# Sorting layer 2 of one entry and layer 3 of another in the same VectorE instructions

## The chip, the cores and the metric

The kernel runs on one core of a Trainium2 chip. The metric is the device time of one execution in microseconds. A core has five engines that work from queues of their own: TensorE (PE in the profile; its weight loads are listed apart as PEld), VectorE (DVE), ScalarE (ACT), GpSimd (POOL) and SyncE (SP), which here only issues DMAs. Each engine takes its instructions in order, and they wait for each other through semaphores.

## What is computed

Sixteen independent entries, each a graph with N = 1024 nodes, C = 64 features a node, and a weighted adjacency matrix of 1024 x 1024. Four layers run one after another, each followed by a residual and a layer norm:

```python
x = layernorm(x + L0(x, adj))                 # adj @ x, two small dense layers, tanh
x = layernorm(x + (adj / clip(adj.sum(2), 1)) @ x)
x = layernorm(x + L2(x, adj, mask))
x = layernorm(x + L3(x, adj, mask))           # as L2, with other weights
```

L2 and L3 aggregate sorted neighbour values:

```python
adj_ = where(eye, 1.0, adj);  nb = (adj_ > 0) & ~eye;  m = nb.sum(-1)
skip = where(m > 10, (m + 1) // 2, 1)
removed = nb & (skip > 1) & (rank % skip == skip - 1)      # rank: place in the row's list of neighbours
valid = where(removed | removed.T, 0, adj_) > 0
s = sort(where(valid[..., None], x[:, None], big), axis=2) # each channel of each node by itself
agg = sum(w * quantile(s, tau) for tau, w in ((.25,.25), (.5,.5), (.75,.25)))
out = relu((x + agg) @ W1 + b1) @ W2 + b2                  # 64 -> 128 -> 64
return out * mask
```

The lists of neighbours depend on the adjacency alone. So layers 2 and 3 of an entry use the same lists, but layer 3 sorts the values that layer 2 has produced.

## The kernel before, in words

**Tiles.** The 1024 nodes of an entry are sorted by their number of neighbours and cut into 8 tiles of 128 nodes (one node a partition). Tile t has room for SIZES[t] values a node: 10, 11, 13, 14, 15, 17, 19, and 33 for tile 7, the *tail*. A tile of values is `got`, 128 x SIZES[t] x 64 in fp32; slot 0 is the node itself, the other slots are its neighbours.

**How a tile is filled.** Tiles 6 to 0 are filled by GpSimd: `fetch` copies slot 0 (L831) and issues one indirect DMA a slot (`gather`, L333), each of which brings 128 rows of 64 values from a table in DRAM (`table[0]` holds x after layer 1, `table[1]` x after layer 2). The tail is filled by `fill`: for each of its 32 slots VectorE makes a one-hot matrix `hot` out of `place` (is_equal), and TensorE multiplies it with the three bf16 parts of x (24 matmuls a slot, `pick`, L329, into `pgk`); ScalarE copies eight slots at a time to `got` (L690).

**How a tile is sorted.** A network of exchanges, laid down ahead by `exchange_plan`. Each step is one VectorE instruction, min or max of two views of `got` and its partner `other`. All VectorE instructions go through a helper, so that they all have line L197 in the profile. Their free size is (slots in the view) x 64: 64 to 1024 elements.

**What follows.** `weigh`: ScalarE multiplies the wanted slots with the weights of the node (L702, `prods`), and VectorE adds them up to `agg`. When a sort's eight tiles are summed, `finish` runs the MLP (`pt`, `ph`, `pd` on TensorE), the residual and the layer norm (`settle`). In layer 2 the result x3s is scattered to `table[1]` by GpSimd (8 indirect DMAs, L747), read back in the nodes' own order by a DMA of SP (L755), and split into three bf16 parts `x3p` (`split`: casts on ScalarE, L361, L365 and L369, with two VectorE subtractions between them). In layer 3 the result x4s is scattered to the output (8 indirect DMAs, L747).

**What is prepared.** `features` computes layers 0 and 1 of an entry: it reads the adjacency twice, a 128-row strip at a time (issued by SP; L403 `px` and L432 `pa` are its matmuls), and makes `near`, the 0/1 matrix of neighbours, on VectorE beside the first reading. `lists` finds the neighbours to be dropped (L484 `pr`), and `left`, the remaining ones with their number; sorts the nodes; and turns the matrix into lists of indices `idx` (L567 `pk`, and maxima of eight on VectorE). `ordered` moves x, place and the weights into the sorted order.

**What sets the order.** The loops are Python generators. The order of the instructions on VectorE, ScalarE and TensorE is written out as they are called (`manual_schedule`); GpSimd and SP get theirs from the framework's scheduler. `Weave` interleaves the generators: each `yield` names a delay, counted in estimated VectorE time, before the generator may go on. The sort itself is the main line; after each of its instructions `catch_up` lets those generators step that are due. `weave.finish(gen)` runs a generator to its end on the spot.

**The main line before.** For each k, `phase(k, 0)` sorts layer 2 of entry k, and `phase(k-1, 1)` sorts layer 3 of entry k-1. At its start a phase completes the filling of its own tail, completes what the filling of the next phase's tail needs, and starts that one. Tiles 6 to 0 are fetched three tiles ahead, into four buffers (`got_s`); there are two tail buffers (`got_l`), five `hot` and three `prods`.

Of the kernel before, what the change touches and what calls it, by code (L numbers as in the profile page):

```python
# [21 lines left out]
P = 128  # L22
# [7 lines left out]
HOTS = 5  # L30
# [59 lines left out]
def cut(t, view, shift=0):  # L90
    s, m, stride, o, length = view
    s += shift
    if m == 1:
        return t[:, s + o : s + o + length, :]
    return t[:, s : s + m * stride, :].rearrange("p (m s) w -> p m s w", m=m)[:, :, o : o + length, :]

# [106 lines left out]
def adj_resnorm_kernel(ctx: ExitStack, tc: tile.TileContext, x, adj_t, nodemask, w01, b01, w02, b02,  # L203
# [20 lines left out]
    off_diag = const.tile([P, P], BF, name="off_diag")  # L224
# [71 lines left out]
    wants = [wanted(low, k) for low, k in zip(LEAST, SIZES)]  # L296
    usual = [exchange_plan(k, want) for k, want in zip(SIZES, wants)]
# [75 lines left out]
    def features(b, e):  # L373
# [3 lines left out]
        near = s.sets.tile([P, NT, N], BF, name="near")  # L377
# [15 lines left out]
        for h in range(NH):  # L393
# [5 lines left out]
            for q in range(G):  # L399
                t = h * G + q  # L400
                rows = slice(t * P, (t + 1) * P)
                for jt in range(NT):
                    nc.tensor.matmul(px[C:, q * P : (q + 1) * P], x_s[:, jt, :], adj[t][:, jt, :], start=jt == 0,  # L403
                                     stop=jt == NT - 1)
                if q == 1:
                    nc.scalar.copy(node_in[:C], px[:C])  # L406
                yield 5
                dve.tensor_scalar(near[:, :, rows], adj[t], 0.0, None, op0=ALU.is_gt)
                dve.tensor_mul(near[:, t, rows], near[:, t, rows], off_diag)
                load(t + 2)  # L410
# [5 lines left out]
            hid_t = s.work.tile([C, HALF], F32, name="hid_t", bufs=1)  # L416
# [7 lines left out]
        e.near = near  # L424
        dve.tensor_add(y, y, b02r[:, None, :].to_broadcast([P, NT, C]))
        yield from settle(x1[:, :, :C], y, "x")
        for h in range(NH):
            pa = s.psum.tile([P, G, C + 1], F32, name="pa", tag="x", bufs=1)
            for q in range(G):
                i = NT + h * G + q  # L430
                for jt in range(NT):
                    nc.tensor.matmul(pa[:, q, :], adj[i][:, jt, :], x1[:, jt, :], start=jt == 0, stop=jt == NT - 1)  # L432
                yield 5
                load(i + 2)
# [4 lines left out]
            dve.tensor_mul(y[:, h * G : (h + 1) * G], pa[:, :, :C], deg[:, 1, :, None].to_broadcast([P, G, C]))  # L439
        x2 = s.feat.tile([P, NT, C], F32, name="x2", tag="x_s", bufs=1)  # L440
# [3 lines left out]
        while b >= 2 and entries[b - 2].tail[0] is None:  # L444
            yield 2
# [4 lines left out]
    def lists(b, e):  # L450
# [26 lines left out]
        for t in range(NT + 1):  # L477
# [8 lines left out]
            yield 4  # L486
            if t:
                for i in range(2):
                    junk = s.work.tile([P, N], BF, name="junk", bufs=1)
                    nc.scalar.activation(junk, prs[t - 1], AF.Sign, bias=lim[:, i, t - 1 : t], scale=-1.0,  # L490
                                         accum_out=cut_at[:, i, t - 1 : t])
            yield 2.5
# [16 lines left out]


        left = s.sets.tile([P, NT, N], F16, name="left")
# [3 lines left out]
        for t in range(NT + 1):  # L515
            if t < NT:
                rows = slice(t * P, (t + 1) * P)
                pv = s.psum.tile([P, N], F32, name="pv", tag="big", bufs=2)
                pvs.append(pv)
# [5 lines left out]
            yield 4  # L525
            if t:
                nc.scalar.activation(left[:, t - 1, :], pvs[t - 1], AF.Relu)  # L527
                junk = s.work.tile([P, N], BF, name="junk", bufs=1)
                nc.scalar.activation(junk, left[:, t - 1, :], AF.Sign, accum_out=key[:, 4, t - 1 : t])
            yield 2  # L530
        e.left = left
# [11 lines left out]
        for t in range(NT):  # L543
            junk = s.work.tile([P, N], BF, name="junk", bufs=1)
# [14 lines left out]
        e.idx = s.feat.tile([P, NT, KS], I32, name="idx", bufs=4)  # L559
        pks, codes, found = {}, {}, []  # L560
        for t in (*reversed(range(NT)), -1, -2, -3):
            if t >= 0:
                pk = pks[t] = s.psum.tile([P, N], F32, name="pk", tag="big", bufs=2)
                for h in range(NH):
                    cols = slice(h * HALF, (h + 1) * HALF)
                    for c in range(NT):
                        nc.tensor.matmul(pk[:, cols], order[:, c, t * P : (t + 1) * P], left[:, c, cols],  # L567
                                         start=c == 0, stop=c == NT - 1)
            yield 4
# [8 lines left out]
            yield 3  # L578
# [13 lines left out]
    def ordered(b, e, order, own):  # L592
# [17 lines left out]
        e.rows = s.feat.tile([P, NT], I32, name="rows", bufs=5)  # L610
        dve.tensor_copy(e.rows, sorted_own[:, :, 1])
        e.out_rows = s.feat.tile([P, NT], I32, name="out_rows", bufs=5)
        dve.tensor_scalar(e.out_rows, sorted_own[:, :, 1], float(b * N), None, op0=ALU.add)
        e.mask = s.feat.tile([P, NT], F32, name="mask_s", bufs=5)
# [3 lines left out]
        yield 7  # L618
        e.xs[0] = s.feat.tile([P, NT, C], F32, name="x2s", bufs=3)
# [9 lines left out]
        while b >= 3 and entries[b - 3].tail[1] is None:  # L629
            yield 2  # L630
        place = s.feat.tile([P, NT, P], F16, name="place", bufs=3)
# [17 lines left out]
        e.none = s.feat.tile([KW - 1, P], BF, name="none", bufs=4)  # L649
        dve.tensor_scalar(e.none, tail_count, nth[: KW - 1], BIG, op0=ALU.is_le, op1=ALU.mult)  # L650
        e.wts = s.feat.tile([P, NT, KW], F32, name="wts", bufs=4)
        hats(e.wts, [P, NT, KW], n1, slot[:, None, :KW].to_broadcast([P, NT, KW]))
# [19 lines left out]
    def fill(e, layer):  # L672

        t = NT - 1
        size = SIZES[t]
        got = s.lists.tile([P, size, C], F32, name="got", tag="got_l", bufs=2)
        nc.gpsimd.tensor_copy(got[:, 0, :], e.xs[layer][:, t, :])
        for g in range(1, size, 8):
            pg = s.psum.tile([P, 8, C], F32, name="pgk", tag="f", bufs=1)
            for k in range(g, g + 8):  # L680
                hot = s.lists.tile([P, NT, P], BF, name="hot", bufs=HOTS)
                dve.tensor_scalar(hot, e.place, float(k), None, op0=ALU.is_equal)
                whole = k < LEAST[t]
                if not whole:
                    nc.tensor.matmul(pg[:, k - g, :], e.none, ident_b[: KW - 1, k - 1 : k].to_broadcast([KW - 1, C]),  # L685
                                     start=True, stop=False)
                pick(pg[:, k - g, :], hot, e.parts[layer], whole)
                yield 3.4
            yield 5
            nc.scalar.copy(got[:, g : g + 8, :], pg)  # L690
            yield 1
        e.tail[layer] = got

    def weigh(e, t, got, agg):

        want = wants[t]
        if t < NT - 1:
            prods = s.lists.tile([P, len(want), C], F32, name="prods", bufs=3)
        else:
            prods = s.lists.tile([P, SIZES[t], C], F32, name="prods_l", tag="other_l", bufs=1)  # L700
        for i, k in enumerate(want):
            nc.scalar.activation(prods[:, i, :], got[:, k, :], AF.Copy, scale=e.wts[:, t, k : k + 1])  # L702
        yield 13
        left = len(want)
        while left > 2:
            more = left // 2
            dve.tensor_add(prods[:, :more, :], prods[:, :more, :], prods[:, left - more : left, :])
            left -= more
        dve.tensor_add(agg[:, t, :], prods[:, 0, :], prods[:, 1, :])
        e.summed += 1  # L710

    def finish(b, e, layer, agg):

        while e.summed < NT:
            yield 1
        e.summed = 0
# [4 lines left out]
        for h in range(NH):  # L721
# [10 lines left out]
            h_t = s.work.tile([H, HALF], F32, name="h_t", bufs=1)  # L732
# [9 lines left out]
        xn = s.feat.tile([P, NT, C], F32, name="x4s" if layer else "x3s", bufs=1 if layer else 2)  # L742
# [9 lines left out]
        if layer == 0:  # L752
            e.xs[1] = xn
            x3 = s.feat.tile([P, NT, C], F32, name="x3", tag="x4s", bufs=1)
            nc.sync.dma_start(x3, dst[:N, :].rearrange("(t p) c -> p t c", p=P))  # L755
            parts = s.feat.tile([P, NT, 3, C], BF, name="x3p", bufs=1)
            yield 35
# [3 lines left out]
    class Weave:  # L761
# [29 lines left out]

        def finish(self, gen):
            while any(w[1] is gen for w in self.works):
                self.advance()

    entries = [SimpleNamespace(near=None, left=None, there=None, listed=False, parts=[None, None], xs=[None, None],
                               tail=[None, None], summed=0) for _ in range(B)]
    weave = Weave()
    preparing, filling, finishing, gots = {}, {}, {}, {}
    allowed = [0]  # L800
    order_of_tiles = [(b, layer, t) for k in range(B + 1) for b, layer in ((k, 0), (k - 1, 1)) if 0 <= b < B
                      for t in reversed(range(NT - 1))]

    def prepare():

        for b in range(B):
            while b > allowed[0] or (b and entries[b - 1].left is None):
# [12 lines left out]
    def fetch(n):  # L820
# [3 lines left out]
        b, layer, t = order_of_tiles[n]  # L824
        e = entries[b]
        if layer:
            weave.finish(finishing[b, 0])
        else:
            prepared(b)
        got = gots[b, layer, t] = s.lists.tile([P, SIZES[t], C], F32, name="got", tag="got_s", bufs=4)  # L830
        nc.gpsimd.tensor_copy(got[:, 0, :], e.xs[layer][:, t, :])  # L831
        for k in range(1, SIZES[t]):
            gather(got[:, k, :], table[layer][b % 3], e.idx[:, t, k - 1 : k])

    def phase(b, layer, following):

        if (b, layer) in filling:
            weave.finish(filling[b, layer])
        nb, nl = following
        if 0 <= nb < B:  # L840
            weave.finish(finishing[nb, 0]) if nl else prepared(nb)
            filling[following] = weave.add(fill(entries[nb], nl))
        if not 0 <= b < B:
            return
        e = entries[b]
        agg = s.feat.tile([P, NT, C], F32, name="agg")
        sums = []
        for t in reversed(range(NT)):
            if t == NT - 1:
                got = e.tail[layer]  # L850
            else:
                fetch(order_of_tiles.index((b, layer, t)) + 3)
                got = gots.pop((b, layer, t))
            other = s.lists.tile([P, SIZES[t], C], F32, name="other", tag="other_l" if t == NT - 1 else "other_s", bufs=1)
            pair = got, other
# [317 lines left out]
```

## Time and profile before

| | before |
|---|---|
| median of 3 runs | 5813.59 us (5813.37 to 5815.44) |
| the profiled execution | 5816.08 us, its span 5814.1 us |
| mean granted TensorE clock | 0.703 |
| VectorE busy | 5256.1 us (90%), 13803 instructions |
| GpSimd busy | 3481.3 us (60%), 3466 instructions |
| TensorE busy, matmuls and weight loads | 3516.2 us (60%), 2698.3 us (46%) |
| ScalarE busy | 1965.9 us (34%) |
| a steady period (one sort of layer 2 and one of layer 3) | 342.3 us |

In a group of the page the number after x counts its instructions; then come busy time in all in us, mean of one in ns, and the idle time of the engine just before them, with what ended most of it. "Issue" is time in which the engine waited for nothing that the profile shows. The profile counts a gather's instruction as busy on GpSimd; the transfer itself lands later, on the DMA queues. A window is a stretch of the span, in us from its start.

### The profile page before, as it was taken

How to read it: one execution, taken by the hardware profiler on the slowest of the kernel's cores; microseconds unless marked ns; L12 is line 12 of the kernel's file. 1: busy time of each engine (PE TensorE's matmuls, PEld its weight loads, DVE VectorE, ACT ScalarE, POOL GpSimd, SP SyncE). 2: the span in 40 equal slices, each digit the busy share in tenths (PEclk: the TensorE clock that was granted, in tenths of full speed). 3: DMA queues.
4: the chain of work that ended last, by engine and by line, in shares of the span. 5: the costliest groups of instructions: out<-in, count | busy, mean ns of one | idle time of the engine just before them, and what ended most of it. 6: DMA issues, size and time to landing. Idle time of an engine off the chain costs nothing. (4 is left out here: it accounts for less than half of the span.)

```text
span 5814.1 us, 110979 instructions
## 1 busy us (share of the span) xinstructions
PE 3516.2 (60%) x43051; PEld 2698.3 (46%) x43144; DVE 5256.1 (90%) x13803; ACT 1965.9 (34%) x4392; POOL 3481.3 (60%) x3466
## 2 busy tenths in 40 slices
PE   6857756666566666657666665666666666634320
PEld 4645544454445445445545544555455545433220
DVE  2766999999999999999999999999999999999977
ACT  4245242333424333242433424243342424312111
POOL 0433275775656576565666656576665657767773
PEclk8978867677667767667776776767767676755565
DMA  2212111212112221211212121121212111111110
GB/s 77 73 44 62 45 34 47 55 40 61 27 46 54 49 56 38 58 30 46 54 41 65 36 48 42 46 55 38 65 33 53 42 46 43 25 19 26 24 27 12
DMA packets 420617, 259.37 MB, mean 45 GB/s; under 512 B 106590, under 2 KB 368878, under 8 KB 420078
## 3 DMA queue, kind: packets, MB, share of 16 engines
q0 software_dynamic: 102400, 105.06, 9.9%
q1 hardware_dynamic: 317678, 147.12, 8.9%
q8 instruction: 339, 5.55, 0.4%
q14 instruction: 200, 1.64, 0.1%
HBM read 239.37 MB, written 12.58 MB: 43 GB/s over the span
## 5 line engine op out<-in xcount | busy, mean ns | idle before, releaser
L333 POOL DMA_INDIRECT got<-table,idx x2944 | 3108.0, 1056 | 1026.0 <-issue 830.8
L329 PEld LDWEIGHTS <-hot 128*128 128x128 bf16 x24576 | 1088.5, 116 | 1880.1 <-DVE hot L197 1832.0
L329 PE MATMUL pgk<-x2p,hot 128*128 128x64 bf16 x12288 | 625.1, 222 | 840.5 <-DVE hot L197 791.2
L329 PE MATMUL pgk<-x3p,hot 128*128 128x64 bf16 x12288 | 588.1, 217 | 753.7 <-DVE hot L197 643.7
L197 DVE TENSOR_TENSOR other<-got 128x256 f32<-128x256 f32 (+10 forms) x2080 | 877.6, 436 | 59.5 <-ACT got L690 16.1
L702 ACT ACTIVATE prods<-got,wts 128x64 f32<-128x64 f32 x1568 | 411.8, 336 | 1384.9 <-DVE got L197 1089.9
L197 DVE TENSOR_TENSOR got<-other 128x256 f32<-128x256 f32 (+8 forms) x1888 | 762.7, 422 | 17.7
L197 DVE TENSOR_TENSOR got<-got 128x256 f32<-128x256 f32 (+6 forms) x1472 | 637.1, 435 | 37.7
L567 PE MATMUL pk<-left,order 128*128 128x512 f16 x2048 | 503.3, 400 | 92.0 <-DVE order L197 89.4
L197 DVE TENSOR_SCALAR hot<-place 128x1024 bf16<-128x1024 f16 x1024 | 449.7, 442 | 27.6 <-PE pgk L329 27.4
L747 POOL DMA_INDIRECT out_dram<-x4s,out_rows x128 | 138.5, 1082 | 511.8 <-DVE x4s L197 456.1
L197 DVE TENSOR_TENSOR other<-other 128x64 f32<-128x64 f32 (+9 forms) x992 | 388.5, 392 | 27.6
L484 PE MATMUL pr<-steps,near 128*128 128x512 bf16 x1443 | 391.4, 420 | 24.5 <-ACT junk L490 16.9
L567 PEld LDWEIGHTS <-order 128*128 128x128 bf16 x2048 | 198.2, 101 | 351.3 <-DVE order L197 119.8
L432 PE MATMUL pa<-x,adj_r 128*128 128x65 f32 x2048 | 295.3, 306 | 86.1 <-issue 76.2
L432 PEld LDWEIGHTS pa<-x,adj_r 128*128 128x128 f32 x2048 | 288.2, 223 | 100.7 <-issue 83.2
L197 DVE TENSOR_TENSOR other<-other,got 128x64 f32<-128x64 f32 (+6 forms) x736 | 305.8, 433 | 10.9
L490 ACT ACTIVATE junk<-pr,nb_st 128x1024 bf16<-128x1024 f32 x256 | 283.7, 1108 | 75.8 <-PE pr L484 55.1
L197 DVE TENSOR_TENSOR got<-got,other 128x64 f32<-128x64 f32 (+4 forms) x960 | 292.3, 319 | 16.0
L523 PE MATMUL pv<-minus_n,takes 128*128 128x128 bf16 x1024 | 268.8, 278 | 48.4 <-DVE takes L197 48.4
L403 PE MATMUL px<-adj_r,x_s 128*64 128x128 f32 x2048 | 285.1, 301 | 4.9 <-ACT node_in L406 2.7
L522 PE MATMUL pv<-scaled,near 128*128 128x128 f16 x1024 | 268.8, 278 | 25.9 <-ACT left L527 25.7
(190 smaller groups left out, 5918.5 us busy)
## 6 DMA issues: line engine op xcount, KB each, us to landing
adj_r<-in_adj_dram SPq DMA_DIRECT2D x256, 512.0 KB
got<-table,idx POOLq DMA_INDIRECT x2944
x_s<-in_x_dram SPq DMA_DIRECT2D x16, 256.0 KB
table<-x SPq DMA_DIRECT2D x16, 256.0 KB
x<-table SPq DMA_DIRECT2D x16, 256.0 KB
table<-x3s,rows POOLq DMA_INDIRECT x128
out_dram<-x4s,out_rows POOLq DMA_INDIRECT x128
table<-no_row SPq DMA_DIRECT2D x6, 0.2 KB
```

The lines of the kernel that those rows point to most:

```text
L197: return call(*args, **kwargs)
L329: nc.tensor.matmul(dst, hot[:, c, :], parts[:, c, q, :], start=first and c + q == 0, stop=c == NT - 1 and q == 2)
L333: nc.gpsimd.indirect_dma_start(out=dst, out_offset=None, in_=tab, in_offset=bass.IndirectOffsetOnAxis(ap=rows, axis=0))
L403: nc.tensor.matmul(px[C:, q * P : (q + 1) * P], x_s[:, jt, :], adj[t][:, jt, :], start=jt == 0, stop=jt == NT - 1)
L432: nc.tensor.matmul(pa[:, q, :], adj[i][:, jt, :], x1[:, jt, :], start=jt == 0, stop=jt == NT - 1)
L484: nc.tensor.matmul(pr[:, h * HALF : (h + 1) * HALF], near[:, c, t * P : (t + 1) * P], steps[:, N - P + h * HALF - c * P :][:, :HALF], star ...
L490: nc.scalar.activation(junk, prs[t - 1], AF.Sign, bias=lim[:, i, t - 1 : t], scale=-1.0, accum_out=cut_at[:, i, t - 1 : t])
L522: nc.tensor.matmul(pv[:, cols], near[:, c, rows], scaled[:, c, :], start=True, stop=False)
L523: nc.tensor.matmul(pv[:, cols], takes[:, c, rows], minus_n, start=False, stop=False)
L567: nc.tensor.matmul(pk[:, cols], order[:, c, t * P : (t + 1) * P], left[:, c, cols], start=c == 0, stop=c == NT - 1)
L702: nc.scalar.activation(prods[:, i, :], got[:, k, :], AF.Copy, scale=e.wts[:, t, k : k + 1])
L747: put = nc.gpsimd.indirect_dma_start(out=dst, out_offset=bass.IndirectOffsetOnAxis(ap=rows[:, t : t + 1], axis=0), in_=xn[:, t, :], in_off ...
```

## The change

There are 18 rounds instead of 32 phases. Round k (`sort_round(k)`) sorts layer 2 of entry k and layer 3 of entry k - 2 together: `got` and `other` get one more dimension of two *members*, and one VectorE instruction works on both. In rounds 0 and 1 there is only layer 2, in rounds 16 and 17 only layer 3. The same holds for the sums of `weigh`; its products on ScalarE and the MLPs of `finish` remain one a member.

What comes with it: tiles are fetched two ahead instead of three, into three buffers for pairs, and the fetch of a tile is issued once the tile before the one being sorted has been weighed (`free`). There is one tail buffer for a pair instead of two single ones, so that the filling for round k + 1 waits until the tail of round k has been summed (`tails_free`); the tail's products are made in place. `hot` has four buffers, `prods` two. At the start of a round the preparation of entry k + 1 and the filling of this round's tail are completed. `near` is now made beside the second reading of the adjacency, in fp16, and `left` is written over it; so `near` of the next entry waits for the last matmul that reads `left` (`packed`). The weights are computed for 21 wanted slots instead of 33. `finish_round` finishes layer 2 first, then layer 3. Some delays of the generators are other ones.

```diff
-HOTS = 5
+HOTS = 4
...
+def cut_pair(t, view, shift=0):
+
+    s, m, stride, o, length = view
+    s += shift
+    if m == 1:
+        return t[:, :, s + o : s + o + length, :]
+    return t[:, :, s : s + m * stride, :].rearrange("p e (m s) w -> p e m s w", m=m)[:, :, :, o : o + length, :]
...
-                dve.tensor_scalar(near[:, :, rows], adj[t], 0.0, None, op0=ALU.is_gt)
-                dve.tensor_mul(near[:, t, rows], near[:, t, rows], off_diag)
                 load(t + 2)
...
+        while b and not entries[b - 1].packed:
+            yield 2
+        near = s.sets.tile([P, NT, N], F16, name="near")
...
+                dve.tensor_scalar(near[:, :, rows], adj[i], 0.0, None, op0=ALU.is_gt)
+                dve.tensor_mul(near[:, t, rows], near[:, t, rows], off_diag)
                 load(i + 2)
...
-        e.wts = s.feat.tile([P, NT, KW], F32, name="wts", bufs=4)
-        hats(e.wts, [P, NT, KW], n1, slot[:, None, :KW].to_broadcast([P, NT, KW]))
+        e.wts = s.feat.tile([P, NT, most_wanted], F32, name="wts", bufs=5)
+        hats(e.wts, [P, NT, most_wanted], n1, want_ids)
...
+    def members(k):
+
+        return [(m, b, entries[b]) for m, b in enumerate((k, k - 2)) if 0 <= b < B]
+
+    def fill(k):
+
+        while k > 0 and not tails_free[k - 1]:
+            yield 1
         t = NT - 1
         size = SIZES[t]
...
+        got = s.lists.tile([P, 2, size, C], F32, name="got", tag="got_l", bufs=1)
+        for m, b, e in members(k):
+            while e.parts[m] is None:
+                yield 1
...
+                    pick(pg[:, i - g, :], hot, e.parts[m], whole)
+                    yield 3.1
+                yield 4
+                nc.scalar.copy(got[:, m, g : g + 8, :], pg)
+                yield 0.5
+            e.filled[m] = True
+        tails[k] = got
...
-            prods = s.lists.tile([P, SIZES[t], C], F32, name="prods_l", tag="other_l", bufs=1)
...
+            prods = got[:, :, want[0] : want[-1] + 1, :]
...
+        free[k, t] = True
         yield 13
...
-            dve.tensor_add(prods[:, :more, :], prods[:, :more, :], prods[:, left - more : left, :])
+            dve.tensor_add(prods[:, which, :more, :], prods[:, which, :more, :], prods[:, which, left - more : left, :])
...
             nc.sync.dma_start(x3, dst[:N, :].rearrange("(t p) c -> p t c", p=P))
+            yield 35
+            while b and not entries[b - 1].filled[1]:
+                yield 2
             parts = s.feat.tile([P, NT, 3, C], BF, name="x3p", bufs=1)
-            yield 35
             yield from split(x3, parts, y)
...
+        k, t = order_of_tiles[n]
+        got = gots[k, t] = s.lists.tile([P, 2, SIZES[t], C], F32, name="got", tag="got_s", bufs=3)
+        for m, b, e in members(k):
+            if m:
+                weave.finish(finishing[b])
+            else:
+                prepared(b)
+            nc.gpsimd.tensor_copy(got[:, m, 0, :], e.xs[m][:, t, :])
+            for i in range(1, SIZES[t]):
+                gather(got[:, m, i, :], table[m][b % 3], e.idx[:, t, i - 1 : i])
...
+    def sort_round(k):
+
+        if k >= 2:
+            weave.finish(rounds[k - 2])
+        weave.finish(filling[k])
+        if k + 1 < B:
+            prepared(k + 1)
+        if k + 1 < B + 2:
+            filling[k + 1] = weave.add(fill(k + 1))
...
+                got, coming = gots.pop((k, t)), order_of_tiles.index((k, t)) + 2
+            other = s.lists.tile([P, 2, SIZES[t], C], F32, name="other", bufs=1)
+            pair = got[:, which], other[:, which]
             for is_max, d, v, i, j, to in usual[t]:
...
+                dve.tensor_tensor(cut_pair(pair[to], v, d if is_max else 0), cut_pair(pair[i], v),
+                                  cut_pair(pair[j], v, d), op=ALU.max if is_max else ALU.min)
                 weave.catch_up()
...
+                if coming is not None and (t == NT - 2 or (k, t + 1) in free):
+                    fetch(coming)
+                    coming = None
...
+        if k:
+            weave.finish(rounds[k - 1])
+        rounds.append(weave.add(finish_round(k, agg, sums)))
```

## The prediction

> **What bounds the kernel now.** I read the page's engine rows first, then its costly groups, then VectorE's groups by form, VectorE's waits, and windows and timelines of single stretches.
>
> ```profile
> span 5814.1 us, 110979 instructions
> PE 3516.2 (60%) x43051; PEld 2698.3 (46%) x43144; DVE 5256.1 (90%) x13803; ACT 1965.9 (34%) x4392; POOL 3481.3 (60%) x3466
> L333 POOL DMA_INDIRECT got<-table,idx x2944 | 3108.0, 1056 | 1026.0 <-issue 830.8
> L747 POOL DMA_INDIRECT out_dram<-x4s,out_rows x128 | 138.5, 1082 | 511.8 <-DVE x4s L197 456.1
> ```
>
> VectorE is busy for 90%. GpSimd (POOL) shows 60%, but its gathers also carry 830.8 us of "issue": a gather is 1.056 us plus 0.28 of issue. Its queue is in order, and it stands 456.1 us before the output scatters, waiting for x4s; the gathers behind them wait too. The waits of VectorE, engine and line first, then total, times, longest:
>
> ```profile
> DVE deg L197 <- PE pa L432: 44.0, 3, 16.5
> DVE own L197 <- ACT junk L529: 36.2, 3, 18.3
> DVE near L197 <- DMA adj_r<-in_adj_dram: 33.9, 8, 7.9
> ```
>
> No gather is in that list: before, every tile is there in time. Next, windows (length, busy time of PE, PEld, DVE, ACT, POOL, granted clock, DMA share, GB/s). The first three are stretches in which VectorE had run out of sorting; the last is one steady period, one sort of layer 2 and one of layer 3.
>
> ```profile
> 194.50:248.50 54.00, 51.80 (x1010) 46.71 (x1011) 25.96 (x71) 9.59 (x15) 35.20 (x36) 0.93 0.40 101
> 483.40:564.30 80.90, 72.99 (x1181) 60.42 (x1186) 33.42 (x88) 55.92 (x92) 38.63 (x42) 0.94 0.26 64
> 5615.60:5655.10 39.50, 34.99 (x810) 31.55 (x810) 20.46 (x51) 7.18 (x16) 30.64 (x33) 0.88 0.15 27
> 2961.10:3303.40 342.30, 222.67 (x2691) 171.68 (x2696) 326.62 (x862) 123.07 (x277) 215.48 (x216) 0.71 0.21 47
> ```
>
> In the last VectorE has only 15.7 us idle in 342.3. In the first three the length is TensorE's work (54.0 for 51.8, 80.9 for 73.0, 39.5 for 35.0). So VectorE bounds the kernel as long as sorting covers TensorE and GpSimd.
>
> **The change, part by part.** *Fewer VectorE instructions.* By form:
>
> ```profile
> L197 DVE TENSOR_TENSOR got<-other 128x256 f32<-128x256 f32 x608 | 242.4, 422 | 6.8
> L197 DVE TENSOR_TENSOR got<-other 128x512 f32<-128x512 f32 x256 | 171.0, 687 | 1.0
> L197 DVE TENSOR_TENSOR got<-other 128x64 f32<-128x64 f32 x480 | 104.1, 222 | 2.0
> L197 DVE TENSOR_TENSOR other<-got 128x1024 f32<-128x1024 f32 x32 | 39.3, 1227 | 1.1
> ```
>
> From 64 to 512 elements the mean goes from 222 to 687 ns: 1.04 ns an element and 155 ns fixed. Two neighbours overlap: count times mean over all forms is 5817 us against 5256 busy, 41 ns for each of 13803. Idle gaps of the steady period add (342.3 - 326.6)/862 = 18 ns. An instruction less saves 155 - 41 + 18 = 132 ns; its elements stay. The order of the two builds has 4396 VectorE instructions fewer, 314 per pair of sorts. That is 580 us in all, 41.4 per pair, and with about 1 us from the narrower weights a round needs 300 us of VectorE instead of 342.
>
> The Trainium skill, "Perfetto Trace Analysis", section "Optimizing Scalar/DVE Operations", gives about 60 ns per DVE instruction on SBUF as data-access overhead and says that grouping helps a saturated engine. By that the whole saving would be 264 us; the rows here say 580, and I go by the rows.
>
> *What sorting no longer covers.* From that price and the build's order I put a clock on VectorE's part of a round (0 is the end of the last sort before): first sort instruction (tail) 66, first subtraction of the x3 split 77, tile 6's sort 145, last x4s 175, tiles 3, 2, 1, 0 at 235, 254, 272, 286, end 300.
>
> (a) TensorE at the border. Preparation of the next entry and the filling of this round's tail are completed before the sort begins. VectorE has 66 us there; TensorE has, in order, 782 pgk matmuls x 0.0494 us (1213.2/24576 on the page's two rows) = 38.6, 128 pk x 0.246 = 31.5, 74 px x 0.139 = 10.3, 192 picks of ordered features x 0.0494 = 9.5, and some 8 for place, transposes and MLP: about 97. Bounds: nothing, if it starts earlier beside the last sort; or 97 x 194.5/124.8 = 151 (the first preparation lasts 194.5 us with 124.8 of TensorE), +85. I take +31, by the three windows above, which are this same situation.
>
> ```profile
> L329 PE MATMUL pgk<-x2p,hot 128*128 128x64 bf16 x12288 | 625.1, 222 | 840.5 <-DVE hot L197 791.2
> L329 PE MATMUL pgk<-x3p,hot 128*128 128x64 bf16 x12288 | 588.1, 217 | 753.7 <-DVE hot L197 643.7
> L567 PE MATMUL pk<-left,order 128*128 128x512 f16 x2048 | 503.3, 400 | 92.0 <-DVE order L197 89.4
> ```
>
> (b) GpSimd at the end of the round. Its queue runs, per round: tiles 6, 5, 4 (96 gathers, both members together), 8 x3s scatters, 8 x4s scatters, tiles 3, 2, 1, 0 (88 gathers). The steady period's GpSimd timeline (start, us, then idle before in brackets):
>
> ```profile
> 3072.19 1.01 POOL L747 DMA_INDIRECT out_dram<-x4s,out_rows  x1 [38.34 <-DVE x4s L197]
> 3073.51 0.98 POOL L747 DMA_INDIRECT out_dram<-x4s,out_rows  x1 [0.30 <-issue]
> ...
> 3083.29 1.01 POOL L333 DMA_INDIRECT got<-table,idx  x1 [0.16 <-issue]
> ...
> 3190.41 0.48 POOL L831 COPY got<-x3s 128x64 f32<-128x64 f32 x1
> ```
>
> From 3083.29 to 3190.41 lie 79 gathers and 5 copies of about 0.45: 1.33 us a gather; where VectorE is quiet 1.25; over the whole run 1.356. A scatter is 1.31, and a gather lands 2.55 us after it (chain of waits). After x4s at 175: 8 scatters 10.5, 88 x 1.33 + 8 x 0.45 = 120.6, landing 2.5: tile 0 is there at 308.6, VectorE wants it at 286: 22 late (15 at 1.25, 25 at 1.356). Before, tiles are loaded three ahead, one sort's at a time, and no tile is late.
>
> (c) GpSimd at the start of the next. It ends tile 0 some 17 us before VectorE ends the round, so at -17. Then 96 x 1.26 + 6 x 0.45 = 123.7 gives 107, the x3s scatters 10.4, and from the last scatter to the first subtraction (load of x3, ScalarE's cast) 5.2 (5580.47 to 5585.63):
>
> ```profile
> 5579.50 0.97 POOL L747 DMA_INDIRECT table<-x3s,rows  x1 [0.30 <-issue]
> ...
> 5585.63 0.69 DVE L197 TENSOR_TENSOR y_m<-x,x3p 128x512 f32<-128x512 f32 x1 [12.13 <-ACT x3p L361]
> ```
>
> So the x3 parts come at 122; VectorE is at that subtraction at 77, or 108 after (a): 14 more, 45 together. Behind it on VectorE stand the filling of the next tail and the sort; SP's adjacency loads stand behind the x3 load. Bounds: 0, if GpSimd gets ahead; 24 more than (a) at 1.356.
>
> *Other edits.* near made in the second adjacency pass: the same VectorE work, 25 us later once (bounds 0 and 25). Fewer hot buffers, tail buffer single, place and rows deeper: in (a); no instruction of their own. Weights of the tail multiplied in place: ScalarE, 34% busy, covers it.
>
> **Sum.** Before: third tail sort starts at 752, the sort of the last-but-one entry's layer 3 at 5470, then 344 to the end. After, the first paired round starts at about 755 (194.5 + 25 for the first preparation, the second preparation up to the border 175, sort 134, border 85, sort 140: taken as equal to before, within 40). A steady round: 300 + 45 + 22.5 = 368. Fourteen paired rounds: the first 383 (more preparation), 370, ten of 368, 369, 367 (the last two have less VectorE work, 272 and 233, and wait for GpSimd instead): 5169. End 344 as before, 2 around the span (5816.1 against 5814.1): 755 + 5169 + 344 + 2 = 6270. The profiled run of before is 5816.1 against a median of 5813.6: no correction.
>
> The Trainium skill, "Perfetto Trace Analysis", section "Identifying the Most-Contended Engine", says to optimise the engine with the highest occupancy first. By that rule, VectorE at 90%, the time would fall to 5235; by the row of the output scatters, where an engine at 60% stands still in an in-order queue, it rises to 6270. This speaks against trusting occupancy here.
>
> **Rivals.** *B: x3 is not late* (GpSimd takes up tile 6 sooner): round 300 + 31 + 22 = 353, last two 347 and 308; about 6000. For: (c) hangs on a 17 us lead. Against: three pairs of buffers allow no earlier start.
>
> *C, the other side: gathers keep up* and only TensorE's 31 us remain: steady rounds 331, short rounds about 320 and 285, about 5680, faster. The deciding point: 454/14 = 32 us less than my round, that is a total lateness per round below about 36. For: GpSimd's work per round is 184 x 1.33 + 16 x 1.31 + 16 x 0.45 = 273, under 300. Against: it must wait for x4s with only 125 us left for 131 of work.
>
> *D: the saving arrives whole:* 5816 - 580 = 5235. Needs (a) to (c) all covered.
>
> *F: preparation at the border goes at its own pace* as in the first 194.5 us: +85 for 31, x3 then in time: 300 + 85 + 22 = 408 a round, about 6830.
>
> **How the numbers follow.** Forecast A 0.58 (6135 at 1.25 a gather to 6450 at 1.356), B 0.17 (5900 to 6135), F 0.10 (6450 to 6900), C 0.11 (5600 to 5800), D 0.02, within 0.2% (12 us, about what a measurement here can tell) 0.02. The range 5900 to 6600 holds A, B and half of F; C, D, no change and the rest of F are left out, 0.20. Faster is C and D, 0.13; same 0.02; slower A, B, F, 0.85.
>
> **What the next profile would show.** Right: about 9400 VectorE instructions, VectorE's busy share under 80%; waits of VectorE on got's gathers (tile 1 or 0, about 20 us a round) and on the x3p cast or x3 load (about 45 with hot's waits on pgk); GpSimd's gathers back to back at 1.25 to 1.33 us and its long stands only before x4s and x3s. Wrong: no wait on gathers (C); stands on ScalarE or adjacency loads at the border (F); an instruction fixed price far from 132 ns would show in steady VectorE busy time, about 290 per round.

## The result, and the profile after

The changed kernel takes 6486.77 us (median of 4 runs, 6471.35 to 6492.52) against 5813.48 us (4 runs): a ratio of 1.1153, 95% interval 1.1134 to 1.1173. It is 673 us slower; 454 were predicted. The profiled execution took 6484.89 us, its span 6483.2 us.

The page of the changed kernel, its engine rows and the groups that answer to those shown of before:

```profile
span 6483.2 us, 106045 instructions
PE 3456.3 (53%) x43095; PEld 2643.7 (41%) x43144; DVE 4729.5 (73%) x9407; ACT 1947.8 (30%) x4394; POOL 3466.9 (53%) x3484
L350 POOL DMA_INDIRECT got<-table,idx x2944 | 3103.2, 1054 | 1032.3 <-issue 850.8
L712 POOL COPY got<-x2s 128x64 f32<-128x64 f32 x16 | 4.7, 296 | 1317.3 <-DVE agg L206 1317.3
```

VectorE has 526 us less to do (5256.1 to 4729.5) in 4396 fewer instructions, 120 ns of busy time each. All of it and 669 us of span have become idle time: 558 us before, 1754 us now. The waits of VectorE say on what (line, total, times, longest):

```profile
DVE other L206 <- DMA got<-table,idx: 413.9, 45, 19.3
DVE y_m L206 <- ACT x3p L378: 310.4, 14, 75.1
DVE hot L206 <- PE pgk L346: 186.2, 131, 5.5
DVE best L206 <- ACT code L601: 114.4, 24, 9.6
```

The first line is new: the first exchange of a tile waits for its gathers. The second was 12.4 us before. One steady round, from the first subtraction of x3 to that of the next round (window; length, busy time of PE, PEld, DVE, ACT, POOL, granted clock, DMA share, GB/s), and the border between two sorts inside a round:

```profile
3253.90:3634.20 380.30, 213.42 (x2693) 162.53 (x2696) 289.45 (x547) 121.95 (x276) 218.85 (x216) 0.72 0.19 43
3123.80:3225.20 101.40, 93.13 (x1406) 68.79 (x1406) 65.34 (x139) 28.60 (x49) 78.61 (x83) 0.96 0.29 68
```

The round is 380 us instead of 342, although VectorE works only 289 of them. Its waits lie where they were forecast, and each is somewhat larger: 28.9 on gathers (22.5 forecast), 18.8 at the x3 split (14), and a border that is 101.4 long for 65.3 of VectorE, so 36 (31).

Now the same round on GpSimd and on VectorE (timelines: start, us, then in brackets the idle time before and who ended it), in order of time:

```profile
3253.94 0.69 DVE L206 TENSOR_TENSOR y_m<-x,x3p 128x512 f32<-128x512 f32 x1 [18.76 <-ACT x3p L378]
```

```profile
3349.60 0.29 POOL L712 COPY got<-x2s 128x64 f32<-128x64 f32 x1 [100.87 <-DVE agg L206]
3350.91 1.58 POOL L786 DMA_INDIRECT out_dram<-x4s,out_rows  x1 [0.85 <-DVE x4s L206]
...
3363.72 0.46 POOL L875 COPY got<-x2s 128x64 f32<-128x64 f32 x1 [0.98 <-issue]
...
3619.16 1.00 POOL L786 DMA_INDIRECT table<-x3s,rows  x1 [0.31 <-issue]
...
3628.11 0.96 POOL L786 DMA_INDIRECT table<-x3s,rows  x1 [0.30 <-issue]
```

```profile
3634.18 0.69 DVE L206 TENSOR_TENSOR y_m<-x,x3p 128x512 f32<-128x512 f32 x1 [17.38 <-ACT x3p L378]
```

This is a closed loop. From the x3 split to x4s VectorE needs 97 us (3253.9 to 3350.9), and GpSimd stands. Then GpSimd runs without a stop: 8 output scatters (12.8), all 184 gathers of a round and their copies (3363.7 to 3619.2: 255.5), 8 scatters of x3s (9.9). Then 5.1 until the next x3 split. 97 + 12.8 + 255.5 + 9.9 + 5.1 = 380.3. VectorE has finished the x3s that these scatters carry at 3592.7, 26 us before the first of them; in the order of the queue they come last.

So two theories fit the profile. *S*, the prediction's sum read term by term: the terms (TensorE at the border, late gathers, late x3) add up, each worth its own size. *L*: the loop through GpSimd's queue alone sets the round, and what lies beside it is worth nothing. And the profile offers a third, *H*: GpSimd stands 1399.5 us in all before the copies into the tail buffer (L712), 101 us in a steady round, with the gathers queued behind it:

```profile
POOL got L712 <- DVE agg L206: 1399.5, 14, 124.9
```

### The profile page after: what moved, and what is told of

Same layout as the page of the kernel before. It is cut to its first block, busy times and chain, and to the rows that moved or that the text cites. A ratio compares the mean times of both kernels' runs of the same rounds, so it can differ in the third digit from the quotient of the medians.

```text
span 6483.2 us, 106045 instructions
## 1 busy us (share of the span) xinstructions
PE 3456.3 (53%) x43095; PEld 2643.7 (41%) x43144; DVE 4729.5 (73%) x9407; ACT 1947.8 (30%) x4394; POOL 3466.9 (53%) x3484
## 5 line engine op out<-in xcount | busy, mean ns | idle before, releaser
L206 DVE TENSOR_TENSOR other<-got 128x512 f32<-128x512 f32 (+12 forms) x1170 | 747.2, 654 | 471.0 <-DMA got<-table,idx 413.9
L712 POOL COPY got<-x2s 128x64 f32<-128x64 f32 x16 | 4.7, 296 | 1317.3 <-DVE agg L206 1317.3
L346 PE MATMUL pgk<-x3p,hot 128*128 128x64 bf16 x12288 | 486.0, 200 | 330.6 <-DVE hot L206 313.6
L206 DVE TENSOR_TENSOR got<-other 128x512 f32<-128x512 f32 (+10 forms) x1062 | 649.5, 630 | 8.4
L206 DVE TENSOR_TENSOR got<-got 128x128 f32<-128x128 f32 (+8 forms) x900 | 587.2, 656 | 22.7
L449 PE MATMUL pa<-x,adj_r 128*128 128x65 f32 x2048 | 391.2, 378 | 356.8 <-DMA adj_r<-in_adj_dram 284.6
L590 PE MATMUL pk<-near,order 128*128 128x512 f16 x2048 | 485.9, 392 | 12.3 <-DVE order L206 12.3
L504 PEld LDWEIGHTS <-near 128*128 128x128 f16 x1536 | 175.4, 116 | 464.2 <-issue 361.2
L206 DVE TENSOR_TENSOR other<-other 128x128 f32<-128x128 f32 (+12 forms) x558 | 321.0, 575 | 16.9
L510 ACT ACTIVATE junk<-pr,nb_st 128x1024 f16<-128x1024 f32 x256 | 281.2, 1104 | 14.6 <-PE pr L504 14.6
L206 DVE TENSOR_TENSOR other<-other,got 128x128 f32<-128x128 f32 (+9 forms) x414 | 259.5, 646 | 7.0
```

Source lines behind the costliest of these rows:

```text
L206: return call(*args, **kwargs)
L346: nc.tensor.matmul(dst, hot[:, c, :], parts[:, c, q, :], start=first and c + q == 0, stop=c == NT - 1 and q == 2)
L504: nc.tensor.matmul(pr[:, h * HALF : (h + 1) * HALF], near[:, c, t * P : (t + 1) * P], steps[:, N - P + h * HALF - c * P :][:, :HALF], star ...
L590: nc.tensor.matmul(cols, order[:, c, t * P : (t + 1) * P], left(c, slice(h * G, (h + 1) * G)), start=c == 0, stop=c == NT - 1)
L712: nc.gpsimd.tensor_copy(got[:, m, 0, :], e.xs[m][:, t, :])
```

## Experiments

All steady rounds below are the mean distance of eight x3 subtractions (rounds 5 to 13). The kernel before ran beside each group of runs, with medians of 5808 to 5812 us. The times of the runs with pace 2.5, 2.2 and "1.9, timed" are medians of four executions; the other experiments ran once, and four executions of the changed kernel lie 21 us apart.

| run | us | steady round |
|---|---|---|
| changed kernel | 6486.8 | 380.0 |
| one part of three in the tail | 6455.9 | 379.2 |
| GpSimd waits for neither x4s nor the tail | 6451.3 | 378.9 |
| 44 gathers a round fewer | 5950.2 | 341.3 |
| four buffers | 6472.2 | 377.8 |
| x3s ahead of tile 4 | 6189.3 | 359.5 |
| four buffers and that order | 5864.0 | 334.5 |
| no forced preparation | 5823.1 | 332.2 |
| tail's filling at 1.9 a slot | 5652.3 | 322.0 |
| at 2.5 a slot | 5927.5 | 344.8 |
| at 2.2 a slot | 5699.6 | 324.2 |
| at 1.9, timed | 5654.6 | 322.2 |

**Is TensorE at the border on the path?**

```diff
-                pick(pg[:, i - g, :], hot, e.parts[m], whole)
+                pick(pg[:, i - g, :], hot, e.parts[m], whole, 1)     # one part of x instead of three
```

> The changed kernel, its tail filled with the first of the three bf16 parts of x only (8 matmuls a slot instead of 24; the low bits of the tail's values are left out). Order of all other work unchanged. Theory S (the three terms of the prediction add up): the TensorE time that the sort no longer covers falls by some 500 matmuls x 0.05 = 25 us a round, so the steady round goes from 381 to about 355 and the time to about 6130. Theory L (the round is one loop through GpSimd's queue: x3's subtraction, 97 us of VectorE until x4s, then 8 scatters, 184 gathers and 8 scatters without a stop, then 5 us to the next x3 subtraction; TensorE is not on it): steady round 376 to 383, the wait on the x3p cast grows from 19 to about 45 us; the time falls only by the first rounds, to 6380 to 6480.

6455.9 us, steady round 379.2. One border and one round of this run, and VectorE's waits in that round:

```profile
2350.30:2444.70 94.40, 82.09 (x891) 55.80 (x891) 66.26 (x137) 28.38 (x49) 73.13 (x78) 0.90 0.30 71
2479.40:2859.90 380.50, 191.02 (x1672) 137.01 (x1672) 289.23 (x547) 121.78 (x275) 219.81 (x216) 0.66 0.18 42
```

```profile
DVE y_m L206 <- ACT x3p L378: 48.4, 2, 24.8
DVE other L206 <- DMA got<-table,idx: 29.1, 3, 11.3
```

1024 matmuls a round are gone and the round keeps its length to 1 us. But the edit took less out of the border than was written down: TensorE's busy time there fell from 93.1 to 82.1 us, and the border is about 95 us long instead of 101.5 (mean of the steady rounds), not 25 shorter. So S, taken with what the edit really removed, asks for a round of 373.5, and 379.2 was measured. The wait at the split took up 6.0 of the 6.5 us (the window counts one at each end: 24.8 a round, against 18.8), as L says. This speaks for L, on 6 us of the 31; the run with four buffers, below, weighs more.

**Do the two waits of GpSimd's queue make the gathers late?**

```diff
-            nc.gpsimd.tensor_copy(got[:, m, 0, :], e.xs[m][:, t, :])
+            nc.scalar.copy(got[:, m, 0, :], e.xs[m][:, t, :])
...
+        if layer:
+            nc.sync.dma_start(out_rows_of[b * N : (b + 1) * N, :].rearrange("(t p) c -> p t c", p=P), xn)
+        for t in range(0 if layer else NT):
```

> The changed kernel, with the two things taken off GpSimd's queue at which it stands 101 us a round: the output goes out by one plain DMA of SP (so its rows stay in sorted order), and the two copies into the tail buffer are made by ScalarE. Theory H (head of line: the gathers of tiles 3 to 0 are late because they stand behind these): the 29 us of waits on gathers go, round 352 or less, time 6080 or less. Theory B (the gathers could not start sooner, because with three pairs of buffers tile 3 needs the buffer of tile 6, which is weighed at about the same moment): round 370 to 384, time 6350 to 6500.

6451.3 us, steady round 378.9: theory B. GpSimd waits longer than before, now for the buffer (waits of GpSimd in this run, then one x3 split on VectorE and the copy behind it on GpSimd):

```profile
POOL got L877 <- ACT prods L740: 2008.5, 18, 273.7
```

```profile
3255.86 0.69 DVE L206 TENSOR_TENSOR y_m<-x,x3p 128x512 f32<-128x512 f32 x1 [18.52 <-ACT x3p L378]
3365.18 0.46 POOL L877 COPY got<-x2s 128x64 f32<-128x64 f32 x1 [114.29 <-ACT prods L740]
```

It now stands before the copy of a tile's slot 0, until ScalarE has weighed the tile that holds the buffer. That copy comes 109.3 us after the x3 split; in the changed kernel it came 109.8 after it (3253.94 to 3363.72), behind x4s and its scatters. The 1399.5 us before L712 were GpSimd's largest wait, and worth about 35 us in all: behind it lay another wait that ended at the same moment. H falls. It also says more exactly what the first leg of the loop is: some 109 us, at whose end both the scatters of x4s and the weighing of the tile that holds the buffer are done. With three buffers, taking the scatters off the queue does not shorten it.

**Is it GpSimd's work at all?**

```diff
+            if m and t <= 3:
+                nc.sync.dma_start(got[:, m, 1:, :], table[m][b % 3][:P, None, :].to_broadcast([P, SIZES[t] - 1, C]))
+                continue
             for i in range(1, SIZES[t]):
```

> The changed kernel, with 44 of the 184 gathers of a round left out: in tiles 3 to 0 the second member's neighbours are not gathered, one plain DMA of SP writes rows of the table there. If GpSimd's queue sets the round (S and L alike): 44 x 1.33 = 58 us less work on it, until VectorE and TensorE set the round at 300 + 31: steady round about 331 to 340, time 5780 to 5920. If it is TensorE's preparation or the delays in the written-out order that set it: steady round above 360, time above 6200.

5950.2 us, steady round 341.3, no wait on gathers left, 8.4 us at the x3 split. The round falls by 38.7 with 58 us of gathers gone; it is as long as the period of the kernel before (342.3). The time is 30 us above the range. The expectation took VectorE and TensorE to be the next limit, but the waits of GpSimd in one round of this run show the same loop, in which it now also stands for buffers:

```profile
POOL got L712 <- DVE agg L206: 99.8, 1, 99.8
POOL got L875 <- ACT prods L740: 13.7, 2, 8.9
POOL got L875 <- DVE other L206: 4.2, 1, 4.2
```

380 less 44 gathers of 1.354, and 17.9 of standing added, is 338 of the 341. That the buffers hold the loop here was worked out from the trace, not tested.

**Is the lateness of tiles 3 to 0 worth its 29 us?**

```diff
-HOTS = 4
+HOTS = 2
...
-        got = ... tag="got_s", bufs=3)
+        got = ... tag=f"got_s{(NT - 2 - t) % 4}", bufs=1)
...
-                got, coming = gots.pop((k, t)), order_of_tiles.index((k, t)) + 2
+                got, coming = gots.pop((k, t)), order_of_tiles.index((k, t)) + 3
```

> The changed kernel with four buffers for pairs instead of three (of 19, 17, 15 and 14 slots) and tiles fetched three ahead; two buffers for hot instead of four, to make room. In the build GpSimd then has, after x4s: tiles 2, 1, 0, then tiles 3, 6, 5, 4 of the next round, then x3s: the 62 gathers of tiles 2 to 0 are early, but all 184 gathers still lie between x4s and x3s. Theory S: the 29 us of waits on gathers go and nothing comes for them: round about 352, time about 6080. Theory L: the loop keeps its length: round 376 to 384, the wait moves from the gathers to the x3p cast (19 to about 45 us or more); time 6400 to 6500.

6472.2 us (within the spread of the changed kernel's own runs), steady round 377.8. Here L is separated most cleanly from S; the largest waits of VectorE in one round of this run (window of 379.0 us):

```profile
DVE y_m L206 <- ACT x3p L378: 43.9, 1, 43.9
DVE hot L206 <- PE pgk L346: 26.6, 12, 7.3
```

The 28.9 us on gathers are gone, and 25 us more are waited at the split. With two buffers for `hot`, VectorE waits 17.7 us more for `pgk` than in the changed kernel's round (8.9); about as much is gone from its other waits at the border (10.6 to 0.7 for `code`, 5.6 to none for `sorted_own`), and the border is 103 us long against 101. So S would still give about 352.

**Shorten the loop and nothing else.** Tile 4's gathers go behind the x3s scatters, into the time in which GpSimd stands:

```diff
+            if layer == 0:
+                last_put[b] = put.ins
...
+            behind = tc.issue_after(last_put[k - 1]) if t in (4,) and k - 1 in last_put else nullcontext()
+            with behind:
```

> The changed kernel with one thing moved on GpSimd's queue: the 28 gathers of tile 4 go behind the scatters of x3s instead of ahead of them, into the time in which GpSimd stands. Theory L: the loop from x3 to x3 becomes 28 x 1.33 + 0.9 = 38 us shorter, 343 us, and is then no longer what sets the round: 300 + 31 for TensorE at the border + 22 to 29 for tiles 3 to 0 = 353 to 360; the waits on the x3p cast go (under 5 us a round). Time 6130 to 6250. Rival (x3 is late because the layer 2 results are, not because of the queue): round stays at 376 or above, time above 6400.

6189.3 us, steady round 359.5, at the upper end of what L gave. 297 us for the place of 28 gathers in a queue. This run alone does not part L from S, which would give 380 - 18.8 = 361 with the x3 wait gone; it shows that the order of the queue makes x3 late, and that it can be cured there. No wait at the split is left in a steady round; the first lines of its waits are now the late gathers, and ScalarE's `code` at the border:

```profile
DVE other L206 <- DMA got<-table,idx: 28.5, 3, 10.7
DVE best L206 <- ACT code L601: 10.6, 2, 9.5
```

If the loop no longer binds, these are worth their size: with four buffers as well, the gathers' 28.5 should go.

**Four buffers and the order.** As the run with four buffers, with tiles 4 and 3 behind the x3s scatters (`t in (4, 3)`; tile 4's fetch is also emitted there).

> The four buffers of the run before, and tiles 4 and 3 behind the scatters of x3s. Loop L: 97 us from x3 to x4s, 8 scatters, 130 gathers, 8 scatters, 5 us: 97 + 10.5 + 130 x 1.33 + 4.5 + 10.4 + 5 = 300. What is left is VectorE's 300 and TensorE's 31 at the border, with more waits of hot (two buffers): steady round 331 to 350, time 5780 to 6000; no waits on gathers, x3p under 5 us a round. If neither queue nor buffers were the cause: round above 370.

5864.0 us, steady round 334.5: within 1% of before. The same four buffers that were worth 2 us a round under the loop are worth 25 without it. (Tile 3's place goes with them in this run; with tile 4 alone moved, the loop was put at 343 us above, and would have bound again.)

**What is left of the border.** Two runs on top, with three buffers for `hot`. The first:

```diff
-        if k + 1 < B:
-            prepared(k + 1)
...
-            while e.parts[m] is None:
+            while e.parts[m] is None or not ready(b):     # ready: its preparation has come to its end
```

> As the run with four buffers and the new order, with three buffers for hot (four instead of five for idx and wts), and without the rule that the preparation of entry k + 1 is completed before the sort of round k begins: TensorE's 97 us at the border can lie beside the sort. If the border's 31 us were TensorE's work without cover: round 305 to 325, time 5450 to 5750, below the kernel before. If they are the tail's filling alone: round 325 to 340.

5823.1 us, steady round 332.2: the preparation being forced, and the third `hot` buffer that this run has besides, are worth 2 us a round together. What stays may be the filling of the tail, paced for a longer round. The second sets its pace:

```diff
-                    yield 3.1
-                yield 4
+                    yield 1.9
+                yield 3
```

> As the run with more under the sort, and the delays of the tail's filling shorter (1.9 instead of 3.1 a slot), so that its last half does not remain for the border. TensorE then has 213 us of work spread over a round of 300: round 302 to 320, time 5400 to 5700; or, if the filling next to the sort makes VectorE wait for TensorE (hot <- pgk), 320 to 340.

5652.3 us, steady round 322.0 in the mean, rounds of 306, 316 and 342 by turns. With this faster filling the kernel is below the one before.

**The pace between.**

> Between the two runs before: four buffers, new order, no preparation forced, the tail's filling at 2.5 a slot (3.1 gave a steady round of 332 us, 1.9 gave rounds of 306 to 342, 321 in the mean). GpSimd's order is here the same in every round. If the border's rest is the filling's last half: a round of 315 to 325, time 5600 to 5700. If the shorter delay only moves VectorE's waits for TensorE (hot <- pgk) into the sort: 330, time about 5800.

5927.5 us (ratio to before 1.0204, 1.0187 to 1.0221), steady round 344.8: the expectation fails, and 2.5 is slower than 3.1 and than 1.9. GpSimd is not the cause (it stands up to 47 us before the x3s scatters, waiting for VectorE); VectorE is idle 55 us in a round, and its largest wait there is TensorE again:

```profile
POOL table L786 <- DVE got L206: 460.8, 12, 47.4
DVE hot L206 <- PE pgk L346: 24.6, 16, 7.8
DVE y_m L206 <- PE pd L776: 6.5, 1, 6.5
```

A pace changes the place of every instruction after it in three written-out orders. 47 of the 55 us (mean of six rounds) lie in stretches of over 30 us without a sort instruction, so between two sorts; which of the moved places costs them was not found.

> The same at 2.2 a slot, GpSimd's order again the same in every round. If the filling at the border is what is left: a round of 308 to 318, time 5520 to 5640, below the kernel before by 3 to 5%. If VectorE's waits move into the sort: 320 to 330, time 5650 to 5800. A round cannot be shorter than VectorE's 290 us busy plus its gaps, 300.

5699.6 us (ratio 0.9811, 0.9795 to 0.9827), steady round 324.2 (315 to 331): in the range of the second case that was written down, but not by its mechanism. Of the 18.9 us a round that VectorE waits for `pgk` (mean of six rounds), 17.6 lie in stretches of over 30 us without a sort instruction, so between two sorts and not in one.

> The kernel of the filling at 1.9 a slot once more, now timed against the kernel before: one run gave 5652 us. If that holds, 5640 to 5665 us, ratio 0.970 to 0.975; it would then be the fastest of all kernels here.

5654.6 us (4 runs, 5647.4 to 5656.7), ratio 0.9732, interval 0.9716 to 0.9748. So sorting in pairs does pay, by 2.7%, with four buffers, another place for two tiles' gathers, a preparation that is not forced, and a faster filling of the tail. Whether the kernel before would gain from a faster filling of its own was not tested; its VectorE is busy for 326.6 us a period, so that without pairing it could not come down to 322. Of VectorE's 342.3 - 300 = 42 us a round that the change can save, the round of 322 has 20.

## Why the prediction was right, and where it was off

*The saving on VectorE* was right: 547 instructions a round against 862, and 289.5 us busy against 326.6, that is 118 ns of busy time an instruction, where 155 - 41 = 114 was priced. (The 18 ns of gaps cannot be read here, since VectorE now waits.) The Trainium skill, "Perfetto Trace Analysis", section "Optimizing Scalar/DVE Operations", gives about 60 ns of engine-busy overhead for one, and about twice that as the latency that a profile shows; here the busy time, in which two overlapping neighbours count once, fell by twice the 60, and the measurement decides.

*(a) TensorE at the border*: 97 us of TensorE forecast, 93.1 measured in a border of 101.4; right in size. In the sum its 31 us lie inside the 45 of (c), which put x3 at 122 whether VectorE stands there at 77 or at 108. The run with a third of the fill's matmuls agrees as far as it goes: 6.5 us less of border, 0.8 less of round.

*(b) and (c)*, the late gathers and the late x3, were right in place and cause. Measured 28.9 and 18.8 against 22.5 and 14. The mis-sized term is the price of a gather: 1.33 and 1.26 us, from stretches of the trace of before. In a steady round 184 gathers and 14 copies of 0.45 take 255.5 us, 1.354 a gather; that is about the 1.356 which stood in the working as a bound. 88 x (1.354 - 1.33) + 96 x (1.354 - 1.26) = 11 us a round, nearly all of the 12 that the steady round (380.0 against 368) is longer. The fourteen paired rounds, 832.9 to 6138.5, take 5306 us instead of 5169.

*The sum* holds the whole loop without naming it: 98 (x3 at 77 to x4s at 175) + 10.5 + 238 + 6.3 of copies + 10.4 + 5.2 = 368, at the prices then taken, the same as 300 + 45 + 22.5. So the round was right, but not its parts one by one. The step that failed is the one that lets the 22.5 of (b) stand beside the 45 of (c) as a term of its own, and takes GpSimd's lead of 17 us over VectorE as given: that lead is made by the wait of (b). When the wait on gathers went (28.9 us, with four buffers), the wait at the split grew by 25 and the round lost 2.2. That is why rival B was wrongly put: "x3 is not late" is not a matter of a lead of 17 us, it takes a shorter loop; when the loop was shortened, the round was 359.5 (B gave 353).

*The start* was off by 78 us: the first paired round begins at 832.9, not at 755. The border before the first sort is 233 us instead of 175, the next one 109 instead of 85:

```profile
208.50:441.90 233.40, 201.52 (x2117) 159.10 (x2120) 89.60 (x206) 82.25 (x124) 19.19 (x22) 0.81 0.26 72
581.10:689.70 108.60, 91.00 (x1069) 67.33 (x1067) 62.51 (x133) 42.50 (x70) 45.64 (x48) 0.88 0.25 63
```

TensorE is busy for 201.5 of the 233: the step "second preparation up to the border 175" was too small; TensorE's work alone is more. What made it so long was not tested. *The end* was right: 344.7 us from the last paired round on, 344 forecast. 832.9 + 5305.6 + 344.7 = 6483.2, the span. The start and the rounds were both put too short (by 78 and 137 us), so that no error hid another.

*The rivals.* C (gathers keep up) comes nearest to the run with 44 gathers fewer: no wait on gathers is left, but the round is 341, not 331, since GpSimd's loop still holds it, and the time is above the kernel before. D never came near. F is excluded: the border keeps TensorE's pace (93.1 us of work in 101.4). The rule to take the engine with the highest occupancy first (the Trainium skill, "Perfetto Trace Analysis", section "Identifying the Most-Contended Engine") did not hold for this change as it was made: VectorE's occupancy fell from 90% to 73%, GpSimd's from 60% to 53%, and the loop through GpSimd's queue made it slower.

## What to carry to other kernels

When two engines wait for each other in turn, close the loop: write down the chain from one event to the same event a round later, and see which of its parts run one after another. While the loop binds, what is not on it is worth next to nothing, however large its wait looks in the profile, and it gets its worth back when the loop no longer binds (four buffers: 2 us a round, then 25). The cheapest cure may be the place of a few instructions in an in-order queue (28 gathers moved: 297 us). Pairing also made each buffer twice as large, and so the prefetch shorter (three buffers instead of four): before pairing, ask whether the prefetch depth survives it.

## What was not expected of the hardware

With 1024 of 2696 matmuls of a round taken away, TensorE's busy time fell by 22 us only (213.4 to 191.0) and the mean granted clock from 0.72 to 0.66. At 0.05 us a matmul, 51 us were to be expected. The fill's matmuls that stayed, a third of them, still took half of the time (34.3 us against 68.3), and others became slower: the mean of `pa` went from 364 to 418 ns, of `px` from 276 to 294, of the `pv` on `near` from 268 to 284. The rows here have the lower clock where TensorE is less busy: 0.96 in the border (93.1 of 101.4 us), 0.72 over the round (213.4 of 380.3), 0.66 in the round with fewer matmuls (191.0 of 380.5). That the clock is what made the others slower fits these rows, but was not tested.
